# Layer 0 of a four-layer graph network on one core: in-degrees from packed adjacency tiles, and layer 3's weight products moved from the front into layer 0's steps

## The chip, the cores and the metric

The kernel runs on one core of one Trainium2 chip, in one launch. The metric is device time in microseconds, the median of several runs of the same kernel. A core has TensorE (PE; its weight loads are shown as PEld), VectorE (DVE), ScalarE (ACT), GpSimd (POOL) and SyncE (SP), which here issues most of the transfers. Each engine takes its instructions in the order in which they stand in its own queue, and waits on semaphores for the others.

## What is computed

The input is x, 2708 nodes by 512 features in f32, and a symmetric 0/1 adjacency matrix adj of 2708 by 2708 in int32, about 2.4% ones and a full diagonal. Four layers follow, each `x = x + layer(relu(layernorm(x)), adj)`. Cut to what matters:

```python
# layer 0
h = relu(layernorm(x));  a = adj.astype(f32)
out = (a.T @ h) @ W0
norm = clip(a.sum(axis=0), 1, None) ** -0.5        # in-degree of each node
x = x + relu(out * norm[:, None])
# layer 1: mean over the first 64 neighbours, two weight products, leaky relu
# layer 2: attention with 8 heads of 64
# layer 3
agg = mask @ h / max(deg, 1)
self_f, nb_f = h @ W_self + b_self, agg @ W_nb + b_nb
x = x + relu(concat(self_f, nb_f) @ W_comb + b_comb)
```

Layer 3 has no nonlinearity between its products, so W_self and W_nb can each be multiplied beforehand with their half of W_comb, and the biases b_self and b_nb too.

## The kernel before, in words

**Chunks and groups.** The 2708 nodes are NC = 22 chunks of 128 rows, the last of 20. The adjacency columns are cut into six groups of chunks, `sizes = [4, 4, 4, 4, 3, 3]`. A unit is a pair (g, m): the block of adjacency rows of chunk m and columns of group g, a tile `ai` of 128x512 (or 128x384) int32, 256 KB. There are 6 x 22 units in order.

**The steps of layer 0.** `staged` (L244) walks over the steps and runs a list of stages, each with a lag: at step s a stage with lag l works on unit s - l.

- lag 0, `load0` (L487): SP loads the adjacency block, into one of ten `ai` buffers.
- only in group 0, `dense` (L264): lag 0 loads the rows of x, lag 1 `norm` (L213: statistics and normalized `hn` on VectorE, the square root on ScalarE), lag 2 `relu_T` (L235: four transposes on TensorE, `hT` written out by ScalarE), lag 3 `product0` (L478): four f32 matmuls with W0, each of which leaves two records in the trace (tile `h_ps`, L186), and `halves` (L285), which splits the result into two parts, one by ScalarE, one by VectorE.
- lag 4, `count0` (L518): ScalarE turns `ai` into the f32 tile `ar` (L523); VectorE runs a scan along the rows (`cum`, L529), keeps the row's running degree (`deg`, L537), and for even m packs two blocks as low and high byte of an int16 tile `two` (L541), which has three buffers.
- lag 5, `sign0` (L553): ScalarE makes a sign count out of `cum` (L557).
- lag 7, `multiply0` (L567): GpSimd issues the store of `two` to the DRAM tile `packed` (L574). TensorE multiplies `ar` with the two halves of h into one PSUM accumulator `acc` for each chunk of the group (L403: 8 or 6 matmuls a unit).

`fenced` (L509) puts `count0` and `sign0` behind the last eviction of the group before, on the same engine. Apart from such edges and from data the build's scheduler decides the order of each queue.

**In-degrees.** For the column sums TensorE also multiplies a column of ones (`oneb`, 32 wide) with the upper 16-bit halves of every `ar` tile (L592), in batches of four tiles at m = 3, 7, 11, 15 and of six at m = 19. ScalarE copies the sums out (`by_col`, L601), and at m = 21 TensorE transposes them (L607), VectorE takes the maximum with 1 (L611), ScalarE the root (L618), VectorE the reciprocal `nrm` (L619). Then `acc` is evicted with that factor, alternately by ScalarE (L645) and VectorE (L640), and GpSimd adds it to x (L648) in all groups but the last.

**Layer 3's weights.** Ahead of all this stands a block of its own (L324 to L375): it loads W_self, W_comb and W_nb; TensorE transposes the two weights (`turn_weight`, L341) and multiplies them with W_comb (`fuse`, L347); VectorE copies the results out (L354); GpSimd stores each of the two as a whole to DRAM (L356). VectorE sums the biases times rows of W_comb into `part` (L367, L369), and TensorE adds over its partitions (L373). Then come the four loads of W0, and layer 0. Layer 3 reads the products much later (`load_l3_weights`).

PSUM has eight banks, shared by all these tiles (`ps`). At the change of group up to four old and four new accumulators exist. x tiles have five buffers.

## Time and profile before

| | before |
|---|---|
| median of 3 runs | 1802.83 us (1800.16 to 1804.46) |
| the profiled execution: time, span | 1800.19 us, 1798.3 us |
| TensorE busy | 1767.9 us, 98% |
| VectorE, ScalarE, GpSimd busy | 1309.7, 816.0, 248.7 us |
| mean granted TensorE clock | 0.995 |
| layer 0's first product; its last | starts at 39.04 us; ends at about 375.9 us |
| column sums (L592) | 484 matmuls from 77.9 to 372.0 us |
| products of layer 3's weights (L347) | 64 records from 7.4 to 36.2 us |

A line of the timeline is: start, duration, engine, source line, operation, written tile, read tiles, shape, number of instructions merged into it, and in brackets how long the engine had been idle and what ended it. A row of the windows is: the stretch, its length, the busy time of PE, PEld, DVE, ACT, POOL with the number of instructions, the granted clock of TensorE, the share of the DMA engines, GB/s. Durations of matmuls overlap in the pipeline, so their cost is read from start to start.

### The profile page before, as it was taken

The numbers are of one execution on the slowest core, as the hardware profiler recorded it, in microseconds if no ns is written. First come the engines' busy times: TensorE is split into PE (matmuls) and PEld (weight loads), VectorE is DVE, ScalarE is ACT, GpSimd is POOL, SyncE is SP. The second block draws the span as 40 slices with busy tenths as digits, with TensorE's granted clock in tenths as the row PEclk, the third lists the DMA queues.
The fourth block names the chain that finished last, engine by engine and source line by source line (L and its number), as shares of the span: only waits on it lengthen the run. The fifth ranks groups of instructions, "written<-read, shape, count | busy, mean of one in ns | idle before, by whom it ended". The sixth has DMA issues, their size and how long they took to land.

```text
span 1798.3 us, 30708 instructions
## 1 busy us (share of the span) xinstructions
PE 1767.9 (98%) x11880; PEld 1050.8 (58%) x11880; DVE 1309.7 (73%) x1842; ACT 816.0 (45%) x1554; POOL 248.7 (14%) x245
## 2 busy tenths in 40 slices
PE   9899999999999999999999999999999999999998
PEld 4456777654448888644454444444444455588786
DVE  4952998855446655888999999999999777633334
ACT  2643777732210000156887767767774566400000
POOL 0101332311111211266000000000001222100000
PEclk9999999999999999999999999999999999999999
DMA  7632666634451211243220121121022444313221
GB/s 251 199 106 71 210 204 192 205 80 119 122 142 50 69 55 47 86 147 123 74 62 25 45 63 44 27 63 50 19 68 60 141 134 133 107 43 99 71 71 40
DMA packets 166445, 176.06 MB, mean 98 GB/s; under 512 B 83454, under 2 KB 105918, under 8 KB 165394
## 3 DMA queue, kind: packets, MB, share of 16 engines
q1 hardware_dynamic: 143738, 130.61, 25.7%
q10 hardware_dynamic: 18808, 33.37, 4.9%
q0 software_dynamic: 3744, 10.03, 1.5%
q8 instruction: 95, 1.56, 0.4%
q14 instruction: 60, 0.49, 0.1%
HBM read 110.60 MB, written 55.36 MB: 92 GB/s over the span
## 4 chain that ended last, share of the span: by engine, by line
PE 86%; DVE 7%; issue 3%; DMA 3%; ACT 1%; POOL 1%; DVEq 0%; SPq 0%; ACTq 0%; POOLq 0%
PE acc L403 33%; PE av L1110 19%; PE nb_ps L186 8%; PE sums L1110 6%; PE wh_ps L186 4%; PE self_ps L186 4%; PE line_ps L186 4%; DVE t L923 3%; PE h_ps L186 3%; PE hT_ps L239 2%; PE fused_ps L347 2%; DVE cum L529 2%; DMA ai<-in_adj 1%; DMA degd<-deg 1%; PE av_ps L1063 1%
## 5 line engine op out<-in xcount | busy, mean ns | idle before, releaser
L923 DVE SCALAR_TENSOR_TENSOR t<-rb,ec,vT 128x2708 f32<-128x2708 f32 (+2 forms) x220 | 529.5, 2461 | 13.2 <-PE sums L1110 8.2
L1110 PE MATMUL av<-t,whs 128*32 128x451 f32 (+3 forms) x4576 | 436.7, 515 | 0.9 <-DVE ln_mv L218 0.9
L403 PE MATMUL acc<-halves,kt 128*128 128x512 f32 x1848 | 433.3, 394 | 2.4 <-DVE kt L777 2.1
L403 PEld LDWEIGHTS acc<-halves,kt 128*128 128x128 f32 x1848 | 345.8, 188 | 86.0 <-DVE kt L777 6.6
L1110 PEld LDWEIGHTS av<-t,whs 128*32 128x32 f32 (+1 forms) x4576 | 166.5, 110 | 198.3 <-issue 170.8
L403 PE MATMUL acc<-halves,ar 128*128 128x512 f32 x924 | 233.3, 405 | 3.3 <-ACT ar L523 2.4
L941 ACT ACTIVATE b<-t,eb 128x2708 bf16<-128x2708 f32 (+3 forms) x91 | 218.0, 2396 | 36.2 <-DVE t L923 34.6
L403 PEld LDWEIGHTS acc<-halves,ar 128*128 128x128 f32 x924 | 170.4, 188 | 52.5 <-issue 6.9
L777 DVE SCALAR_TENSOR_TENSOR kt<-lastr,index,vT 128x512 fp32r<-128x512 int16 (+3 forms) x154 | 111.4, 735 | 75.9 <-PE acc L403 75.5
L220 ACT ACTIVATE ln_rs<-ln_mv,eps 128x1 f32<-128x1 f32 x88 | 25.4, 292 | 295.0 <-DVE ln_mv L218 285.6
L1349 DVE CAST kt<-vT 128x512 fp32r<-128x512 uint8 (+3 forms) x154 | 56.4, 368 | 138.2 <-PE acc L403 138.2
L1077 POOL TENSOR_SCALAR z<-y 128x512 f32<-128x512 f32 x22 | 44.1, 2004 | 655.3 <-DVE y L1070 646.4
L1110 PE MATMUL sums<-t,whs 128*32 128x338 f32 (+4 forms) x1464 | 131.7, 449 | 0.8 <-ACT out L1151 0.8
L529 DVE TENSOR_TENSOR_SCAN cum<-ai,deg 128x512 int16<-128x512 int32 (+2 forms) x110 | 128.0, 1176 | 0.5 <-DMA ai<-in_adj 0.5
L911 ACT ACTIVATE whs<-wh,ef 128x64 f32<-128x64 f32 x220 | 76.5, 348 | 99.4 <-PE sums L1110 47.6
L557 ACT ACTIVATE cum<-cum,limit 128x512 int16<-128x512 int16 (+3 forms) x132 | 88.0, 667 | 55.8 <-DVE deg L537 54.9
L1110 PEld LDWEIGHTS sums<-t,whs 128*32 128x32 f32 (+1 forms) x1464 | 54.6, 109 | 62.2 <-issue 32.2
L216 DVE BATCH_NORM_STATS2 ln_st<-x 128x6 f32<-128x512 f32 x88 | 60.2, 684 | 35.6 <-DMA x<-x 22.5
L186 PE MATMUL h_ps<-w0s,hT 128*128 128x512 f32 x168 | 78.5, 611 | 2.3 <-DVE deg L537 1.4
L186 PE MATMUL nb_ps<-wfn,hT 128*128 128x512 f32 x168 | 78.5, 611 | 2.1 <-ACT hT L241 2.1
L241 ACT ACTIVATE hT<-hT_ps 128x512 f32<-128x512 f32 x88 | 51.8, 589 | 54.4 <-PE hT_ps L239 52.8
L523 ACT ACTIVATE ar<-ai 128x512 fp32r<-128x512 int32 (+2 forms) x132 | 74.9, 567 | 2.4 <-DMA ai<-in_adj 2.4
(202 smaller groups left out, 1911.9 us busy)
## 6 DMA issues: line engine op xcount, KB each, us to landing
x<-x SPq DMA_DIRECT2D x105, 256.0 KB
ai<-in_adj SPq DMA_DIRECT2D x84, 256.0 KB
x<-x ACTq DMA_DIRECT2D x84, 256.0 KB
x<-in_x SPq DMA_DIRECT2D x42, 256.0 KB
rb<-rT SPq DMA_DIRECT2D x7, 1354.0 KB
wh<-whd SPq DMA_DIRECT2D x70, 96.0 KB
packed<-two POOLq DMA_DIRECT2D x44, 128.0 KB, 3.7
whd<-wh SPq DMA_DIRECT2D x21, 256.0 KB
```

Of the source, the lines that this page charges most:

```text
L186: nc.tensor.matmul(po[:n], lhsT[:, f, :n], w[:, f, :], start=(f == 0), stop=(f == NF - 1))
L216: nc.vector.bn_stats(st[:n], xc[:n])
L403: nc.tensor.matmul(acc[:R], weight[:, k * R : (k + 1) * R], parts[:, i, :], start=(m == 0 and i == 0), stop=(m == NC - 1),)
L523: nc.scalar.activation(ar[:, :gw], ai[:, :gw], AF.Square, accum_out=squares[:R, m, g : g + 1])
L529: nc.vector.tensor_tensor_scan(cum[:n, :gw], ai[:n, :gw], ai[:n, :gw], 0.0 if g == 0 else deg[:n, m : m + 1], op0=ALU.add, op1=ALU.max,)
L557: nc.scalar.activation(cum[:n, :gw], cum[:n, :gw], AF.Sign, bias=limit[:n], scale=-1.0, accum_out=signs[:n, m, g : g + 1],)
L777: nc.vector.scalar_tensor_tensor(by_chunk(kt, cs), lastr[:, cs[0] * R : (cs[-1] + 1) * R].rearrange("p (c r) -> p c r", r=R), index[:R, m ...
L911: ins = nc.scalar.activation(t[:q, :O], wh.pop((u, m))[:q], AF.Copy, scale=by)
L923: ins = nc.vector.scalar_tensor_tensor(t[:q, : hi - lo], row[h][:q, lo:hi], ec[:q, m, h : h + 1], vT[g][:q, k, lo:hi], op0=ALU.max, op1=AL ...
L941: nc.scalar.activation(b[:q, : hi - lo], weight[s][:q, : hi - lo], AF.Sigmoid, bias=eb[:q, m, h : h + 1], scale=STEEP,)
L1110: nc.tensor.matmul(p[j * S : (j + 1) * S, : b - a], lhsT, rhs[:, part * size + a : part * size + b], start=(s % NC == 0), stop=(s % NC == ...
L1349: nc.vector.tensor_copy(by_chunk(kt, cs), pattern(m, cs))
```

## The change

Both parts lie in layer 0.

*In-degrees.* In `count0`, GpSimd adds up the packed tiles `two` of row chunks 0 to 18 of a group as 32-bit integers, one add for each even m from 2 on (tile `total`; no byte overflows with ten tiles of zeros and ones). At m = 20 VectorE adds the low and high bytes into a bf16 tile `by_row`. At m = 19 of the multiply stage TensorE multiplies, for each chunk of the group, three stationary tiles (`by_row` and the upper halves of the last two `ar` tiles) with one column of ones: 12 or 9 matmuls of one column a group, whose result stands with nodes on partitions, so that the copy and the transpose go. The maximum, root and reciprocal follow there and not at m = 21. `two` has four buffers.

*Layer 3's weights.* The block in front goes. SP issues x chunk 0, half of W_self, x chunk 1, the other half, and W0; TensorE transposes W_self there. W_comb's halves, W_nb and the biases are loaded in the steps, W_comb's first half and the biases from step 12 of group 0. The products go one matmul at a time into the steps of groups 1 and 2 (W_self), and the transposes and products of W_nb into those of groups 3 and 4. ScalarE, not VectorE, copies the products out, and each quarter is stored by itself. The bias row is summed by VectorE in the last steps ahead of groups 1 and 3 and closed in group 5. `count0` and `sign0` of the first 20 units also stand behind the normalized `hn` of the chunk two ahead (VectorE) and the `hT` of the chunk one ahead (ScalarE).

In the instruction queues as built, SP has the loads x0, ws, ws, x1, ws, ws, four w0s, then adjacency and x in turn, and W_comb's first half with the biases around x chunks 12 and 13. TensorE has 16 transposes of W_self, 8 of chunks 0 and 1, product 0, the transposes of chunk 2, product 1, and so on. VectorE has the first four bias operations behind the normalization of chunk 9 and in front of the halves of chunk 5.

```diff
@@ norm, relu_T
-        nc.vector.tensor_scalar(hn[:n], xc[:n], mv[:n, 0:1], rs[:n], ...)
+        normed.append(nc.vector.tensor_scalar(hn[:n], ...).ins)
...
+        evicted.append(nc.scalar.activation(hT[:, :, :n], pt[:, :, :n], AF.Relu).ins)
@@ front
-    with tc.tile_pool(name="pre", bufs=2) as pre:
-        ws = [load_weight(pre, w_self, "ws")]
-        wc = load_weight(pre, w_comb, "wc", k=2 * NF)
-        ws.append(load_weight(pre, w_nb3, "ws"))
...
-        turn_weight(0)
-        for f in range(NF):
-            if f == NF // 2:
-                turn_weight(1)
-            fuse(0, f)
-        for f in range(NF):
-            fuse(1, f)
...
+    class Fusion:
...
+        def turn(self, i, f):
+            if f == 0:
+                self.wsT[i] = self.pool.tile([P, NF, D], F32, name="wsT")
+            pt = ps.tile([P, NF, P], F32, name="wsT_ps", tag="ps")
+            for k in range(NF):
+                nc.tensor.transpose(pt[:, k, :], self.ws[i][:, f, k * P : (k + 1) * P], ident)
+            nc.scalar.copy(self.wsT[i][:, :, f * P : (f + 1) * P], pt)
+
+        def multiply(self, i, f, k):
+            if k == 0:
+                self.po[i, f] = ps.tile([P, D], F32, name="fused_ps", tag="ps")
+            po = self.po[i, f]
+            nc.tensor.matmul(
+                po,
+                self.wsT[i][:, k, f * P : (f + 1) * P],
+                self.wc[i][:, k, :],
+                start=(k == 0),
+                stop=(k == NF - 1),
+            )
+            if k == NF - 1:
+                wf = self.pool.tile([P, D], F32, name="wf", bufs=1)
+                nc.scalar.copy(wf, self.po.pop((i, f)))
+                nc.gpsimd.dma_start(fused[i][f * P : (f + 1) * P, :], wf)
@@ fenced
-                        for ins in fences.values():
+                        early = ()
+                        if i < NC - 2:
+                            early = normed[i + 2], evicted[i + 1]
+                        for ins in (*fences.values(), *early):
@@ count0
-                    two = wk.tile([R, WG + P - R], I16, name="two", bufs=3)
+                    two = wk.tile([R, WG + P - R], I16, name="two", bufs=4)
...
+                    if m == 0:
+                        pairs[g] = two
+                    elif m < NC - 2:
+                        total = pairs[g]
+                        if m == 2:
+                            total = wk.tile([R, WG], I16, name="total", bufs=1)
+                        nc.gpsimd.tensor_tensor(
+                            total[:, :KR].bitcast(I32),
+                            pairs[g][:, :KR].bitcast(I32),
+                            two[:, :KR].bitcast(I32),
+                            ALU.add,
+                        )
+                        pairs[g] = total
+                    else:
+                        both = pairs.pop(g)[:, :KR].bitcast(mybir.dt.uint8)
+                        both = both.rearrange("p (w e) -> p e w", e=2)
+                        by_row = by_rows[g] = wk.tile([R, WG], BF16, name="by_row", bufs=1)
+                        nc.vector.tensor_tensor(by_row[:, :KR], both[:, 0], both[:, 1], ALU.add)
@@ multiply0
-                for j in batch:
-                    q = rows(j)
-                    for k in range(K):
-                        nc.tensor.matmul(
-                            sums[g][k * 32 : (k + 1) * 32, :R],
-                            oneb[:q],
-                            uppers[j][:q, 2 * k * R + 1 : 2 * (k + 1) * R : 2],
...
+                if m == NC - 3:
+                    by_row = by_rows.pop(g)
+                    uppers = [(by_row, 1, R)]
+                    uppers += [(tiles[i + j][0].bitcast(BF16), 2, rows(m + j)) for j in (1, 2)]
+                    pt = ps.tile([P, KMAX], F32, name="sums_ps", tag="ps")
+                    for k in range(K):
+                        for j, (upper, e, q) in enumerate(uppers):
+                            nc.tensor.matmul(
+                                pt[:R, k : k + 1],
+                                upper[:q, e * k * R + e - 1 : e * (k + 1) * R : e],
+                                oneb[:q, :1],
+                                start=(j == 0),
+                                stop=(j == len(uppers) - 1),
+                            )
@@ the steps
+            def load_first(i):
...
+                load(0)
+                fusion.load_ws(0, half=0)
+                load(1)
+                fusion.load_ws(0, half=1)
+                w0_of.append(load_weight(weights, w0, "w0s", tag="w"))
+                for f in range(NF):
+                    fusion.turn(0, f)
...
+            for i in range(2):
+                first_unit = (1 + 2 * i) * NC
+                at(first_unit - 10, fusion.load, i)
+                steps = [(fusion.turn, i, f) for f in range(NF) if i]
+                steps += [(fusion.multiply, i, f, k) for f in range(NF) for k in range(NF)]
+                for g, own in enumerate((steps[: len(steps) // 2], steps[len(steps) // 2 :])):
+                    for n, step in enumerate(own):
+                        at(first_unit + g * NC + 2 + n * (NC - 5) // len(own), *step)
+                for k in range(NF):
+                    at(first_unit - 4 + k, fusion.add, i, k)
+            at(5 * NC + 2, fusion.close)
...
             staged(
                 len(units),
+                (0, load_first),
                 (0, load0),
-                *[first_dense(lag, fn) for lag, fn in dense(x_in, product0, rows_of=paired)],
+                *first[1:],
                 (4, fenced(count0)),
                 (5, fenced(sign0)),
                 (7, save0),
                 (7, multiply0),
+                (7, fuse0),
             )
```

## The prediction

> **What bounds the kernel now.** I read the page's busy line first, then the stretches of layer 0 (windows), then TensorE's timeline at the two places where it idles, then the rows of the pieces that the change touches.
>
> ```profile
> PE 1767.9 (98%) x11880; PEld 1050.8 (58%) x11880; DVE 1309.7 (73%) x1842; ACT 816.0 (45%) x1554; POOL 248.7 (14%) x245
> ...
> 39.00:164.00 125.00, 120.38 (x462) 67.83 (x464) 72.39 (x146) 57.09 (x147) 9.46 (x18) 0.97 0.41 133
> ...
> 173.70:216.90 43.20, 43.20 (x263) 33.36 (x262) 39.52 (x59) 32.16 (x92) 13.37 (x16) 1.00 0.66 205
> ...
> 303.20:340.80 37.60, 34.26 (x199) 25.12 (x197) 31.65 (x64) 26.84 (x92) 13.32 (x19) 1.00 0.55 172
> 340.80:375.90 35.10, 34.02 (x203) 25.69 (x202) 26.10 (x82) 22.12 (x87) 11.66 (x22) 1.00 0.40 115
> ```
>
> TensorE is busy 1767.9 of 1798.3 us, so moving work that it must still do gains only what it now idles or runs slowly; only removing work gains more. In layer 0 (rows: length, then PE, PEld, DVE, ACT, POOL busy, clock, DMA) it idles 4.6 us in group 0 with its dense steps (125.0 - 120.38), nothing in groups 1 to 3 (43.2 us each, VectorE at 39.5), 3.3 in group 4 and 1.1 in group 5. The front:
>
> ```profile
> 3.64 3.88 PE L341 MATMUL wsT_ps<-ident,ws 128*128 128x128 f32 x16 [3.64 <-DMA ws<-in_L_gnn_W_self]
> ...
> 14.30 1.91 PE L341 MATMUL wsT_ps<-ident,ws 128*128 128x128 f32 x16
> ...
> 16.05 20.77 PE L347 MATMUL fused_ps<-wc,wsT 128*128 128x512 f32 x48
> ...
> 39.04 3.70 PE L186 MATMUL h_ps<-w0s,hT 128*128 128x512 f32 x8 [0.25 <-ACT hT L241]
> ```
>
> The first product of layer 0 starts at 39.04. A matmul of these weights has two records: 20.77/24 = 0.865 us each, 32 of them 27.7 us. Later in group 0 TensorE waits for a normalized chunk that stands behind scans on VectorE:
>
> ```profile
> 82.84 1.11 PE L239 MATMUL hT_ps<-ident,hn 128*128 128x128 f32 x4 [2.50 <-DVE deg L537]
> 84.29 6.14 PE L186 MATMUL h_ps<-w0s,hT 128*128 128x512 f32 x8 [0.34 <-ACT hT L241]
> ...
> 86.00:88.00 2.00, 2.00 (x4) 0.80 (x3) 2.00 (x5) 0.41 (x1) 0.00 (x0) 0.50 0.35 135
> ```
>
> VectorE is busy all of that row, and the clock granted after the 2.5 us wait is 0.50: the eight records take 6.14 instead of 3.6 us, the transposes 1.11 instead of 0.60, so 3.0 us more are lost.
>
> **The part taken away: column sums on TensorE.** One batch of four tiles costs the gap between two products:
>
> ```profile
> 222.67 0.42 PE L592 MATMUL sums_ps<-ar,oneb 128*32 128x128 bf16 x16
> 223.02 1.20 PE L403 MATMUL acc<-halves,ar 128*128 128x512 f32 x4
> ...
> 211.55 0.64 PE L592 MATMUL sums_ps<-ar,oneb 128*32 128x128 bf16 x24
> 212.12 3.99 PE L403 MATMUL acc<-halves,ar 128*128 128x512 f32 x16
> ```
>
> Start to start: 0.35 us for 16, 0.57 for the last 24. A group has four of the first and one of the second, and one transpose of 0.11: 2.08 us, in the three-chunk groups (0.34 for 12) 2.04. Six groups: 12.4 us.
>
> In their place stand 66 pairs of a 128-column weight load and a one-column matmul (12 in a four-chunk group, 9 in the others). No row of before has that pair. Below: 0.35/16 = 0.022 us a pair, as the 32-column loads show (1.5 us in all). Above: 0.11, the pace of the L239 transposes (four in 0.44 us), which load 128 columns too (7.3 us); if each waited out its own load and its result, as rows of small matmuls with 0.19 + 0.18 us durations have it, 24 us. I take 0.08, near the transposes because the load has their width but half their bytes: 5.3 us. Net -7.1 us.
>
> GpSimd gets nine adds a group (54) of 128x256, or 128x192, int32. The nearest row is its own add of 128x512 f32:
>
> ```profile
> L648 POOL TENSOR_TENSOR x<-x,y x19: 1283/1702/2210, 175.5 to 345.9; 128x512 f32<-128x512 f32 x19
> ...
> 307.06 3.27 DVE L529 TENSOR_TENSOR_SCAN cum<-ai,deg 128x384 int16<-128x384 int32 x2
> ...
> 310.30 1.53 DVE L541 SCALAR_TENSOR_TENSOR two<-ai 128x384 int16<-128x384 int32 x1
> ```
>
> Half of 1702 ns is 0.85 us, 7.7 a group; below 0.6, above 1.7 if the integer form costs double. With the page's 13.4 us a group and the packed stores in the same queue GpSimd stays under half busy, and nothing that it feeds is due before the by_row add of row chunk 20, two chunks after the last sum: free on GpSimd. But these adds slow VectorE. While four adds ran from 305.07 to 311.41, two scans took 3.27 instead of 1.91 us and a pack 1.53 instead of 0.54: 2.4 us lost in 6.3, a share of 0.38, or 2.9 us a group. The Trainium skill (SBUF — State Buffer, section on the two separate sides) makes it harsher: the pair that VectorE and GpSimd share is an exclusive lock for a whole instruction, against a VectorE op with two SBUF inputs too, so all 7.7 us would be lost. The trace shows longer scans, not full exclusion. By the trace VectorE needs 39.5 + 2.9 + 0.6 (by_row, at a pack's price) = 43.0 us in groups 1 to 3, by the rule 47.8. TensorE there will need 43.2 - 2.1 + 1.0 + 6.9 (eight products) = 49.0 (group 3: six products and 1.9 us of transposes, 49.2). So both cost nothing behind the moved products; without that cover (42.1 us) the rule would cost 5.7 us a group, the trace 0.9. Group 4: VectorE 31.65 + 0.5 + 2.2 to 5.8, under TensorE's 34.3 + 8.7 - 1.3. Group 5 has no products: 26.1 + 0.5 + 2.2 to 5.8 = 28.8 to 32.4 against 34.
>
> The divisor is now made at row chunk 19, so the 0.9 us chain transpose, max, root, reciprocal before the evictions goes. TensorE did not wait for it: zero.
>
> **The part moved: layer 3's weights.** In front stay 16 transposes of W_self (1.9 us), done while layer 0's weights come in. Into groups 1 to 4 go the 32 products (27.7), 16 transposes (1.9) and into group 5 the bias product (0.9): 30.5 us of TensorE, none hidden, since groups 1 to 3 have no gap. VectorE loses eight evictions of 0.68 us to ScalarE (0.58 each; it has 11 us a group free). The partial bias (four ops of 0.7) stands on VectorE inside the dense steps and waits for the combining weights and bcol, which SP issues right behind x chunk 13. In before bcol landed some 4 us after its issue; VectorE's 9 us of work since the release of chunk 13 cover that. Behind it queue the halves of chunk 5, which TensorE wants two steps later: zero, at most 2 us if the cover fails. SP's 22 issues (8 ws, 8 wc, biases) go in among x and adjacency loads at 0.5 us each, with steps of 6 us: zero. GpSimd's eight stores, 0.54 to 0.99 us, stand before packed stores; nothing waits. An accumulator bank for a product is wanted at row chunk 2, some 4 us after the group's start, by when the old four are evicted (last at 220.04 for a group that ended at 216.9): 0 to 1 us a group, in the allowance below.
>
> **The new front.** SP issues x0, half of ws, x1, half of ws, four w0s. Before, loads 5 to 8 (wc) were taken up at 7.33, 7.98, 8.73 and 9.59; w0s is now loads 7 to 10, so the first product starts at about 8.7 instead of 39.04. In the order of the built kernel the transposes of chunk 2 stand before product 1; x2 is load 12, lands near 11.5 to 12, and its chain (statistics 0.69, 0.17, root 0.29, 0.15, normalize 0.54, hand-overs) ends near 14.2, while product 0 ends near 12.2: a wait of 2.0. After that the new fences put a scan behind the normalize of the chunk two ahead, and VectorE's step of 3.9 us (2.2 dense, 1.7 count) fits into TensorE's 6: the 4.6 us of waits and 3.0 of slow clock go.
>
> Here a rule speaks against the change. At its start the trace shows a clock of 1.00 from the first transpose on after 3.6 us without work. The Trainium skill (TensorE: Matmul & The Clock Gate, Part 1) has half rate as the default and after an idle window of about 3.4 us, and a warm-up of about 3.4 us. The old front warmed up on work that had to wait for nothing; the new one has sparse transposes and a 2 us wait at 12. By the trace's start it costs 0; by the rule, and by 82.8 to 89.3, up to 3.0. I take 1.5.
>
> **The sum,** on the profiled execution (span 1798.3, time 1800.19). From the first product (39.04) to layer 0's last (375.94): 336.9 us. Less idle 4.6 + 3.3 + 1.1, clock 3.0, sums 12.4: 312.5. Plus pairs 5.3, moved work 30.5: 348.3. Plus new losses: wait at chunk 2 2.0, clock 1.5, groups 1 to 5 together 1.5: 353.3. From 8.7 on, layer 0 ends at 362.0 instead of 375.9: 13.9 us less. Nothing behind it changes. On the profiled run 1786.3, on the median 1802.83, which is 2.6 higher, 1788.9. The profiled one is at the fast end of 1800.16 to 1804.46, so I say 1788.
>
> **The rivals.** (A) As above, 62%: 1782 to 1794 from the pair at 0.022 to 0.11 and losses of 2 to 10 us. (B) The front starves, 16%: x and adjacency share SP, VectorE hits the partial bias too early, a wait of 3 us or more brings the half clock several times; two such spells at 2.5 + 3.0 (as at 82) take 5 to 11 us back: 1794 to 1801. For it: one such wait now costs that; against it: the new fences. (C) Slower, 5%: the integer adds on GpSimd shut VectorE out. Its slack after by_row is 8.8 us in each of groups 1 to 3, 9.4 in group 4, 7.0 in group 5; at a blocked time b per wide add (three quarters of it per narrow one) the excess is 27b - 26.4 + 13.5b - 16.4, the whole gain of 13.9 from b = 1.40 us. At 1.7 (full-size row, wholly exclusive) it takes 26 us: 1814. Against it: 0.85 from the row and the 0.38 share. (D) More, 14%: pairs at 0.03, no slow clock, no wait at chunk 2: 1776 to 1782. (E) The change moves nothing in time, 3%: pairs pay the whole of 12.4 us and the front's start is lost to loads: 1800 to 1805.
>
> About 0.2% (3.6 us) is what a measurement of this kernel can tell from no change. Faster: A, D and 14 of B's 16: 0.90; same: 2 of B and E: 0.05; slower: C: 0.05. Range 1779 to 1797: A, 8 of D's 14 and 10 of B's 16, so 8 in 10.
>
> **What would show it.** The first h_ps record near 9 us; a gap of about 2 us before chunk 2's transposes; no wait on L561 in group 0, clock 1.00 past 15 us. L630: start to start 1.0 us for 12 pairs. Groups 1 to 3 at 49 us with PE full and VectorE at 43 to 48; group 4 about 42, group 5 about 34. GpSimd's L581 near 0.85 us. Layer 0's last product near 362. Wrong if L581 takes over 1.4 us with scans stretched alike, if the L630 pairs take over 0.2 us, or if the first dense steps show clock 0.50 for over 5 us.

## The result, and the profile after

| | before | after |
|---|---|---|
| median (range), same chip | 1803.12 us (1800.16 to 1804.46) | 1793.95 us (1792.77 to 1796.16) |
| ratio, 95% interval | | 0.9953 [0.994, 0.9966] |
| the profiled execution: time, span | 1800.19, 1798.3 us | 1793.95, 1792.2 us |
| layer 0's first product starts | 39.04 us | 11.15 us |
| layer 1's first product (`nb_ps`) starts | 376.32 us | 363.06 us |
| layer 1's aggregation (`acc<-halves,kt`) starts | 536.84 us | 531.04 us |

The change saves about 9 us, where 14.8 were forecast (1788; range 1779 to 1797). In the two profiles, layer 0 ends 13.3 us earlier, close to the forecast 13.9. Then 7.5 us are given back between layer 1's first product and its aggregation (160.52 us before, 167.98 after), and what follows takes the same time (1261.5 and 1261.2 us).

The busy line of after's page, and its windows by group (rows: stretch, length, busy time of PE, PEld, DVE, ACT, POOL with instructions, clock, DMA share, GB/s):

```profile
PE 1755.0 (98%) x11456; PEld 1044.4 (58%) x11456; DVE 1323.0 (74%) x1840; ACT 815.7 (46%) x1555; POOL 301.0 (17%) x305
```

```profile
11.15:135.70 124.55, 124.43 (x448) 73.56 (x449) 80.71 (x170) 60.82 (x162) 14.46 (x23) 1.00 0.50 163
135.70:183.90 48.20, 48.20 (x201) 35.99 (x200) 43.03 (x61) 32.75 (x93) 23.86 (x27) 1.00 0.64 201
183.90:232.10 48.20, 48.20 (x201) 36.02 (x201) 40.57 (x57) 30.50 (x86) 23.84 (x27) 1.00 0.68 211
232.10:288.70 56.60, 50.61 (x213) 37.83 (x212) 47.95 (x70) 36.15 (x104) 23.48 (x26) 0.97 0.52 164
288.70:329.60 40.90, 39.90 (x160) 28.66 (x159) 34.17 (x67) 28.42 (x98) 22.05 (x31) 1.00 0.59 185
329.60:362.60 33.00, 32.58 (x144) 24.78 (x144) 29.71 (x81) 21.39 (x83) 20.68 (x34) 1.00 0.48 140
362.60:392.00 29.40, 23.92 (x61) 11.02 (x60) 12.03 (x30) 5.30 (x12) 1.87 (x3) 0.88 0.35 80
```

Groups 0, 1 and 2 have TensorE full at clock 1.00. Two rows stand out: group 3 (232.10 to 288.70), where TensorE idles 6.0 us, and the first 29 us of layer 1, where it idles 5.5 us at a clock of 0.88. These are the two places to explain.

**Group 3.** TensorE's timeline, and VectorE's at the same place:

```profile
235.58 0.73 PE L423 MATMUL acc<-halves,ar 128*128 128x512 f32 x2 [1.89 <-DVE nrm L638]
...
249.27 3.63 PE L423 MATMUL acc<-halves,ar 128*128 128x512 f32 x8 [3.76 <-ACT ar L547]
```

```profile
232.31 3.15 DVE L387 SCALAR_TENSOR_TENSOR part<-wc,bcol,part 128x512 f32<-128x512 f32 x4 [4.94 <-DMA wc<-in_L_gnn_W_comb]
235.37 0.15 DVE L638 TENSOR_SCALAR nrm<-sums_ps 128x4 f32<-128x4 f32 x1
...
242.36 5.29 DVE L553 TENSOR_TENSOR_SCAN cum<-ai,deg 128x512 int16<-128x512 int32 x2
```

The second half of the partial bias (W_nb's four operations, L387) waits 4.94 us for W_comb's second half, which SP issues only at 227.66 us, behind eleven adjacency loads. The divisor (L638) is queued behind it. It reads `sums_ps` and so frees that bank of PSUM. TensorE has by then issued six products, two for each of three new accumulators, while group 2's four are not yet evicted: the fourth new one waits 1.89 us for the divisor. The evictions queue behind it too, and VectorE is then late: two scans next to GpSimd's four additions to x take 5.29 us (two such scans without neighbours: 2.43 us, at 235.89), ScalarE's sign counts wait for them with `ar` behind, and TensorE waits 3.76 us more, after which eight products take 3.63 us at half clock instead of 2.13. At the start of group 1 the same scans take 5.29 us too (at 139.95) and TensorE waits for nothing; there VectorE was not late.

**Layer 1's start.** VectorE, then ScalarE, then TensorE, in after:

```profile
372.61 0.18 DVE L758 TENSOR_SCALAR rcnt<-rdeg 128x22 f32<-128x22 f32 x1 [12.76 <-DMA rdeg<-degd]
...
373.38 0.45 DVE L233 TENSOR_SCALAR hn<-x,ln_mv,ln_rs 128x512 f32<-128x512 f32 x1
```

```profile
373.94 0.20 ACT L641 ACTIVATE nrm<-nrm 128x3 f32<-128x3 f32 x1 [13.96 <-DVE nrm L638]
```

```profile
373.89 0.66 PE L244 MATMUL hT_ps<-ident,hn 128*128 128x128 f32 x4 [3.80 <-DVE hn L233]
376.22 6.70 PE L186 MATMUL nb_ps<-wn,hT 128*128 128x512 f32 x8 [1.68 <-ACT hT L246]
```

and VectorE and TensorE at the same place before:

```profile
381.22 0.18 DVE L695 TENSOR_SCALAR rcnt<-rdeg 128x22 f32<-128x22 f32 x1 [12.40 <-DMA rdeg<-degd]
```

```profile
383.63 3.60 PE L186 MATMUL nb_ps<-wn,hT 128*128 128x512 f32 x8
...
392.38 0.66 PE L239 MATMUL hT_ps<-ident,hn 128*128 128x128 f32 x4 [1.28 <-DVE hn L230]
```

The node degrees go to DRAM and come back in another layout (`degd`, `rdeg`), for the divisors of layers 1 and 3 (`rcnt`, four small operations). VectorE meets them right after layer 0's last scans and waits 12.4 us before, 12.8 after. The third `hn` of layer 1 (chunk 2) is queued behind, and TensorE's first wait (3.80 us) is for it. Layer 0's last divisor is queued there too: ScalarE waits 13.96 us for it, with the `hT` of layer 1's chunk 1 behind, and that is TensorE's second wait (1.68 us). Before, VectorE started its last scan at 366.6 us and TensorE still had 9.3 us of layer 0 to do (to 375.9). After, it starts that scan at 357.65 with TensorE at 5.0 us from the end (362.6). The wait is as long; its cover has shrunk. Idle 3.80 + 1.68 and, at half clock, 6.70 instead of 3.60 us: 8.6 us, against 1.28 before; the difference, 7.3, is the 7.5 given back.

### The profile page after: what moved, and what is told of

It reads as the page before. It is cut to its first block, busy times and chain, and to the rows that moved or that the text cites. A ratio compares the mean times of both kernels' runs of the same rounds, so it can differ in the third digit from the quotient of the medians.

```text
span 1792.2 us, 29931 instructions
## 1 busy us (share of the span) xinstructions
PE 1755.0 (98%) x11456; PEld 1044.4 (58%) x11456; DVE 1323.0 (74%) x1840; ACT 815.7 (46%) x1555; POOL 301.0 (17%) x305
## 4 chain that ended last, share of the span: by engine, by line
PE 82%; DVE 9%; DMA 3%; issue 3%; ACT 1%; POOL 1%; SPq 0%; DVEq 0%; POOLq 0%; ACTq 0%
PE acc L423 31%; PE av L1173 19%; PE nb_ps L186 8%; PE sums L1173 6%; PE self_ps L186 4%; PE line_ps L186 4%; PE wh_ps L186 3%; DVE t L986 3%; PE h_ps L186 3%; DVE cum L553 2%; PE hT_ps L244 2%; PE fused_ps L369 1%; DMA x<-in_x 1%; DMA degd<-deg 1%; DMA ai<-in_adj 1%
## 5 line engine op out<-in xcount | busy, mean ns | idle before, releaser
L423 PE MATMUL acc<-halves,ar 128*128 128x512 f32 x924 | 249.3, 420 | 7.4 <-ACT ar L547 5.0
L553 DVE TENSOR_TENSOR_SCAN cum<-ai,deg 128x512 int16<-128x512 int32 (+2 forms) x110 | 143.2, 1318 | 0.0
L186 PE MATMUL nb_ps<-wn,hT 128*128 128x512 f32 x168 | 78.7, 612 | 1.7 <-ACT hT L246 1.7
L186 PE MATMUL wh_ps<-w2s,hT 128*128 128x512 f32 x168 | 75.8, 593 | 0.0
```

The source lines that it names most:

```text
L186: nc.tensor.matmul(po[:n], lhsT[:, f, :n], w[:, f, :], start=(f == 0), stop=(f == NF - 1))
L423: nc.tensor.matmul(acc[:R], weight[:, k * R : (k + 1) * R], parts[:, i, :], start=(m == 0 and i == 0), stop=(m == NC - 1),)
L553: nc.vector.tensor_tensor_scan(cum[:n, :gw], ai[:n, :gw], ai[:n, :gw], 0.0 if g == 0 else deg[:n, m : m + 1], op0=ALU.add, op1=ALU.max,)
```

## The experiments

Each ratio is against the kernel before on the same chip, with its 95% interval. The first four runs, the next four and the last three each shared a chip.

| kernel | median us | ratio to before |
|---|---|---|
| W_nb's bias operations later | 1788.26 | 0.9934 [0.992, 0.9949] |
| divisors `rcnt` later | 1789.55 | 0.994 [0.9925, 0.9955] |
| both moves | 1781.19 | 0.9898 [0.9883, 0.9912] |
| before, with `rcnt` later | 1799.33 | 0.9995 [0.9986, 1.0003] |
| the change again | 1795.0 | 0.9966 [0.9955, 0.9977] |
| in-degree part alone | 1815.33 | 1.0084 [1.007, 1.0099] |
| front part alone | 1788.03 | 0.9932 [0.9918, 0.9945] |
| the change without the early fences | 1805.84 | 1.0028 [1.0018, 1.0039] |
| both moves, again | 1778.91 | 0.9879 [0.9864, 0.9894] |
| front part alone, both moves | 1786.8 | 0.9924 [0.991, 0.9937] |
| the change, GpSimd's adds left out | 1783.11 | 0.9893 [0.9878, 0.9909] |

### The two waits of VectorE, each moved

**W_nb's bias operations later** (12 units later, and behind group 2's evictions on VectorE):

```diff
+            def add_behind(i, k):
+                with tc.issue_after(fences["dve"]):
+                    fusion.add(i, k)
...
-                    at(first_unit - 4 + k, fusion.add, i, k)
+                    at(first_unit - 4 + k + 12 * i, add_behind if i else fusion.add, i, k)
```

> The changed kernel with one edit: the four bias operations of W_nb's half are traced twelve units later and stand on VectorE behind the evictions at the start of group 3. Theory W (VectorE waits 4.94 us for the second half of W_comb, and the divisor and evictions of group 2 queue behind it): group 3 falls from 56.6 to 48 to 49 us, no half clock there, and the time falls by 6 to 9 us against the changed kernel's 1794, to about 1786. Rival G (the integer adds on GpSimd shut VectorE out in group 3): group 3 stays over 54 us and the time within 2 us of 1794. Rival L (the gain is given back at the start of layer 1, where TensorE waits for the row degrees anyway): group 3 is short, but the time falls by under 3 us.

Measured: layer 1's first product starts at 355.77 instead of 363.06 us. The stall in group 3 is gone (0.81 us of waiting is left); the waits at layer 1's start are there as in the change (3.76 and 1.67 us, then eight products in 6.43).

**The divisors `rcnt` later** (their four operations stand behind the normalization of layer 1's chunk 8):

```diff
-        nc.vector.tensor_scalar(rcnt, rdeg, float(NEIGHBORS), 1.0, op0=ALU.min, op1=ALU.max)
-        nc.vector.reciprocal(rcnt, rcnt)
-        nc.vector.tensor_scalar(rdeg, rdeg, 1.0, None, op0=ALU.max)
-        nc.vector.reciprocal(rdeg, rdeg)
...
         staged(NC, *stages1, done=len(AHEAD))
+        with tc.issue_after(normed[NC + 8]):
+            nc.vector.tensor_scalar(rcnt, rdeg, float(NEIGHBORS), 1.0, op0=ALU.min, op1=ALU.max)
+            nc.vector.reciprocal(rcnt, rcnt)
+            nc.vector.tensor_scalar(rdeg, rdeg, 1.0, None, op0=ALU.max)
+            nc.vector.reciprocal(rdeg, rdeg)
```

> The changed kernel with one edit: the four VectorE operations that turn the row degrees into rcnt and rdeg stand behind the normalization of layer 1's chunk 8. Theory D (VectorE waits 12.8 us for the round trip of the degrees through DRAM, and the normalization of layer 1's chunk 2 queues behind it, after which TensorE runs at half clock): the waits of 3.80 and 1.68 us and the slow products (6.70 instead of 3.60) at 374 to 383 us go, and the time falls by 6 to 8 us, to 1786 to 1788. Rival X (the x1 rows of layer 1 are late anyway): TensorE waits elsewhere between 370 and 400 us and the time falls by under 3 us.

Measured: layer 0 ends as in after (layer 1's first product at 362.70), the wait is gone, and layer 1's aggregation starts at 522.42 instead of 531.04 us.

**Both moves:**

> Both edits together: bias operations of W_nb behind the evictions of group 2, and rcnt and rdeg behind layer 1's chunk 8. If W and D are separate waits, the gains add: 13 to 16 us below the changed kernel, 1778 to 1781. If one gives the other back, it is within 3 us of the better of the two single edits.

**Before, with the divisors later:**

> The kernel before with the edit on rcnt and rdeg alone. Theory D says that the same 12.4 us wait on VectorE costs almost nothing there, because TensorE still has 7 to 9 us of layer 0 left when it begins: only the 1.28 us idle before chunk 3's transposes can go, so 1801.5 to 1803.5, no change. If instead it gains over 4 us, the wait was costly before as well, and the changed kernel did not uncover it.

Measured up to the start of layer 1's aggregation, the moves save 7.6 us (523.44), 8.6 us (522.42) and together 15.5 us (515.51): they add, so these are two separate losses. The divisors' move leaves the kernel before unchanged (0.9995), although the wait that it removes is just as long there: before, it was covered. So the loss in layer 1 is due to the cover that the change took away, not to the wait as such. The whole times say it less cleanly. Against the change's ratios of 0.9953 and 0.9966 (the change did not run on this chip), W_nb's move gains 3 to 6 us where 6 to 9 were expected, the divisors' 2 to 5 where 6 to 8 were, and both 10 to 12 where 13 to 16 were.

The profiled executions show where a part of the gain goes. From the aggregation's start to the end those of the two single moves need some 1266.5 us, those of after, of before and of both moves 1261 to 1263. Of the 5 us to after, 3.5 lie in layer 2's attention (from its first product to layer 3's first: 555.9 and 555.8 us, against 552.4). It is the clock. TensorE has the same waits there, one of 2.49 us and later two of 0.94 and 1.83, but more half clock follows them in the single moves. Around the first the clock is 0.83 in after (986 to 996 us) and 0.66 in W_nb's move (979 to 989); around the other two, after and then W_nb's move:

```profile
1380.00:1389.02 9.02, 6.25 (x83) 2.92 (x75) 7.81 (x17) 5.79 (x10) 2.42 (x2) 1.00 0.23 69
1374.50:1385.45 10.95, 8.19 (x82) 3.38 (x74) 9.70 (x19) 5.91 (x10) 4.36 (x3) 0.81 0.29 83
```

The remaining 1.7 us are a product of layer 3 that takes 5.40 instead of 3.70 us after a wait (one as slow, 5.25 us, stands in both moves). Two executions of one and the same kernel differ in this way too (after, in its second run, shows a clock of 1.00 at the first of these waits), so this is no loss that the moves are shown to cause.

The windows of both moves (second run; group 3, layer 1's start):

```profile
232.10:281.20 49.10, 48.30 (x214) 36.84 (x213) 45.20 (x69) 34.15 (x97) 24.12 (x26) 1.00 0.58 186
355.20:385.00 29.80, 29.71 (x84) 13.78 (x82) 14.79 (x31) 5.96 (x13) 3.11 (x3) 1.00 0.50 108
```

Group 3 takes 49.10 us, as the prediction had it, and layer 1 starts with TensorE full.

### One part alone, and the fences

**The change again:**

> The changed kernel without any edit, on the chip on which the parts are timed, as their common reference. From its ratio of 0.9953 it stands 8.4 us below the kernel before, with group 3 at 56 to 57 us and the wait at layer 1's chunk 2 again.

Measured: 6.1 us below before, not 8.4; the two intervals overlap. The waits are much the same (1.84, 0.22 and 3.75 us in group 3, 3.92 and 1.22 at layer 1's start).

**The in-degree part alone** (the kernel before, with the GpSimd adds, `by_row` and the one-column products; the weights stay in front, no early fences):

```diff
-                    two = wk.tile([R, WG + P - R], I16, name="two", bufs=3)
+                    two = wk.tile([R, WG + P - R], I16, name="two", bufs=4)
...
+                        nc.gpsimd.tensor_tensor(
+                            total[:, :KR].bitcast(I32),
+                            pairs[g][:, :KR].bitcast(I32),
+                            two[:, :KR].bitcast(I32),
+                            ALU.add,
+                        )
...
-                for j in batch:
...
+                if m == NC - 3:
+                    by_row = by_rows.pop(g)
```

> The kernel before with the in-degree part alone (adds on GpSimd, one-column matmuls, four buffers of two). There the moved products no longer cover VectorE. Theory S (a share of about 0.38 of GpSimd's add time is lost on VectorE): VectorE needs some 43 us in groups 1 to 3, TensorE only 41.4, so these groups stay at 42.5 to 43.5 us, and the time falls by 2 to 6 us from group 0, 4 and 5. Rival R (the shared pair is locked for whole instructions): groups 1 to 3 take 47 us or more and the time rises by 5 us or more. Rival F (adds cost VectorE nothing): groups at 41.4 us and the time falls by 9 to 11 us.

Its windows (group 0 with the dense steps, then groups 1 to 3, which lasted 43.2 us each before):

```profile
39.00:174.00 135.00, 128.58 (x449) 75.05 (x450) 74.38 (x150) 59.88 (x157) 20.78 (x26) 0.97 0.41 130
174.00:218.20 44.20, 42.07 (x186) 32.84 (x185) 41.00 (x60) 30.45 (x86) 22.82 (x25) 1.00 0.63 201
218.20:265.00 46.80, 42.99 (x185) 34.15 (x185) 43.60 (x61) 32.34 (x94) 22.81 (x25) 0.96 0.63 197
265.00:312.60 47.60, 44.25 (x185) 35.06 (x185) 44.38 (x66) 32.98 (x96) 22.81 (x25) 0.93 0.60 183
```

TensorE has less to do and the groups get longer: it now waits for ScalarE's `ar` (12.2 us in all of layer 0, the longest 3.8), which comes behind VectorE's scans, and runs part of the time at a lower clock. VectorE's queue shows the bound. These are all its longer waits in one round from an eviction to the same eviction of the next group:

```profile
223.75 0.75 DVE L641 TENSOR_SCALAR y<-acc,nrm 128x512 f32<-128x512 f32 x1 [2.03 <-POOL x L649]
252.32 0.69 DVE L569 TENSOR_TENSOR by_row<-total 128x512 bf16<-128x512 uint8 x1 [0.56 <-POOL total L558]
264.16 0.18 DVE L620 RECIPROCAL nrm<-nrm 128x4 f32<-128x4 f32 x1 [0.27 <-ACT nrm L618]
270.09 0.75 DVE L641 TENSOR_SCALAR y<-acc,nrm 128x512 f32<-128x512 f32 x1 [2.03 <-POOL x L649]
```

A round takes 46.3 us (the one before it, from 177.40, too): 43.1 of work and 3.2 of waiting, nearly all of it for GpSimd and none for TensorE. So groups and time come out near what rival R said (47 us or more, the time up), but not by R's 7.7 us of lost VectorE time a group. With the wait at layer 1's start grown too (165.6 us to the aggregation instead of 160.5), the part by itself makes the kernel 14 us slower.

**The front part alone** (the change with before's column sums: no GpSimd adds, `two` with three buffers):

```diff
-                        nc.gpsimd.tensor_tensor(
-                            total[:, :KR].bitcast(I32),
...
-                if m == NC - 3:
-                    by_row = by_rows.pop(g)
...
+                for j in batch:
+                    q = rows(j)
+                    for k in range(K):
+                        nc.tensor.matmul(
+                            sums[g][k * 32 : (k + 1) * 32, :R],
+                            oneb[:q],
```

> The changed kernel with the column sums of before (484 matmuls on TensorE, divisor at row chunk 21, two with three buffers), so the moved weight products and the new front alone. The front still gains some 8 us (first product at 11 instead of 39 us, 30.5 us of products later, the waits and the half clock of group 0 gone), the stall of group 3 remains at 6 to 9 us, TensorE has some 11 us more to do, and is later at layer 1, so that the wait for the row degrees shrinks to under 3 us. Together 0 to 4 us below the kernel before. If the sums part was the whole gain, it is slower than before by 2 us or more.

```profile
137.20:187.30 50.10, 50.10 (x280) 36.43 (x279) 39.15 (x59) 33.22 (x94) 14.44 (x18) 1.00 0.61 194
187.30:237.20 49.90, 49.90 (x279) 36.28 (x278) 42.26 (x63) 33.21 (x94) 14.43 (x18) 1.00 0.68 216
```

The expectation (0 to 4 us below before) failed: it is 13 us below. Its wide groups take 50.0 us, 1.8 more than the change's, all on TensorE. Yet it beats the whole change by 7 us (1788.03 and 1795.0 on one chip), because group 3 has no stall (50.0 us as well) although VectorE waits 3.6 us for W_comb there too, and layer 1's start costs 161.1 us instead of 168. Without the adds VectorE is far enough ahead to afford both waits.

**The change without the early fences:**

```diff
-                        if i < NC - 2:
-                            early = normed[i + 2], evicted[i + 1]
```

> The changed kernel without the two new fences (a scan may stand ahead of the normalization two chunks on). If these fences removed the waits of group 0 (1.4, 2.5 us and 3.0 us of half clock in before), waits for normalized chunks come back in the first 120 us and the time rises by 3 to 8 us against the changed kernel. If the order of the loads alone did it (x and adjacency in turn, so that scans are not ready in a bunch), group 0 still takes 124 to 126 us and the time is within 1.5 us of the changed kernel.

The expected waits came back, and cost more than the 3 to 8 us expected. The first product starts at 13.55 us, and the window of group 0 has 5 us without work:

```profile
13.55:147.10 133.55, 128.31 (x449) 75.05 (x450) 80.55 (x168) 61.15 (x160) 19.19 (x23) 0.97 0.45 144
```

Group 0 takes 133.55 us instead of 124.55. The two fences are worth 11 us, more than the whole change brings: without them it would be slower than before (1.0028).

### The square, and the adds by themselves

**Both moves again, and the front part alone with both moves:**

> The whole change with both moves (W_nb's four bias operations later, the divisors rcnt/rdeg of layers 1 and 3 later). Theory: the two waits of VectorE are what the change lost; without them the time is about 1781, 12 to 14 us below the change, and layer 1's aggregation starts near 515.5. Rival (the gain of the two moves is chance of one chip): 1787 to 1790.

> The front part alone (column sums on TensorE as in before) with the same two moves. This completes a square of four: in-degree part yes or no, moves yes or no. Theory: without GpSimd's adds VectorE has a lead of its own and the moves are worth little, about 1.5 us, to some 1786.5; the in-degree part, worth minus 7 without the moves, is then worth plus 5 to 9 us with them (1.8 us of TensorE a wide group). Rival (the in-degree part costs more than it brings in any case): 1776 to 1780, below the whole change with the moves.

| ratio to before | without the moves | with both moves |
|---|---|---|
| front part | 0.9932 | 0.9924 |
| front and in-degree part | 0.9966 | 0.9879 |

The moves are worth 1 us where there are no adds (the intervals overlap), and 10 to 16 us where there are (0.9953 and 0.9966 to 0.9898 and 0.9879). The in-degree part costs 7 us without the moves and brings 8 us with them (1786.8 to 1778.91). The version with both parts and both moves is the fastest of all that ran: 1778.91 us.

**The change without GpSimd's adds** (`by_row` from the last packed tile alone):

```diff
                     elif m < NC - 2:
-                        total = pairs[g]
-                        if m == 2:
-                            total = wk.tile([R, WG], I16, name="total", bufs=1)
-                        nc.gpsimd.tensor_tensor(
-                            total[:, :KR].bitcast(I32),
-                            pairs[g][:, :KR].bitcast(I32),
-                            two[:, :KR].bitcast(I32),
-                            ALU.add,
-                        )
-                        pairs[g] = total
+                        pairs[g] = two
```

> The whole change, with GpSimd's nine adds a group left out: by_row is made from the last packed tile alone, so the in-degrees lack rows 0 to 2303; all the rest is as in the change. Theory (the adds stretch VectorE's scans and so use up its lead): scans of 128x512 go back from 1.52 to about 1.34 us, the wait for W_comb's second half ahead of group 3 stays at 3 to 5 us but costs TensorE 0 to 3 us instead of 8.7, the wait of layer 1's start is covered as in before; 1783 to 1788. Rival 1 (the two waits are there whatever the adds do): 1792 to 1796. Rival 2 (GpSimd shuts VectorE out for whole adds, 7.7 us a group): VectorE's busy time in groups 1 and 2 falls from 43 to about 35 us rather than to 40.

The scans from 130 to 360 us by shape (count, then busy time and mean ns of one), before, after, and with the adds left out:

```profile
L529 DVE TENSOR_TENSOR_SCAN cum<-ai,deg 128x512 int16<-128x512 int32 x60 | 79.3, 1337 | 0.0
```

```profile
L553 DVE TENSOR_TENSOR_SCAN cum<-ai,deg 128x512 int16<-128x512 int32 x62 | 93.1, 1520 | 0.0
```

```profile
L553 DVE TENSOR_TENSOR_SCAN cum<-ai,deg 128x512 int16<-128x512 int32 x62 | 81.4, 1332 | 0.0
```

1520 ns with the adds, 1337 and 1332 without: the adds stretch a wide scan by 0.18 us in the mean, 4.0 us a group of 22. Its windows of groups 1 to 3:

```profile
135.60:183.60 48.00, 48.00 (x201) 36.11 (x201) 39.43 (x62) 32.97 (x93) 14.47 (x18) 1.00 0.64 202
183.60:231.60 48.00, 48.00 (x201) 36.09 (x200) 40.13 (x62) 31.38 (x89) 14.45 (x18) 1.00 0.71 223
231.60:281.20 49.60, 48.47 (x213) 36.70 (x213) 41.24 (x66) 35.42 (x103) 13.91 (x17) 1.00 0.57 176
```

VectorE still waits for W_comb (5.6 us in all), but group 3 loses 1.1 us of TensorE instead of 6.0. VectorE's load in group 1 falls from 43.0 to 39.4 us, not to 35: rival 2 took 0.85 us for each add, which is twice what an add costs VectorE (the part on the prediction shows it). Layer 1's start is only partly cured (1.03 and 1.68 us of waits, the clock stays full), which the expectation had not allowed for. In groups 1 and 2, behind the moved products, the adds cost TensorE 0.2 us each. Of their price of 12 us in the whole change (1795.0 and 1783.11, with before at 1801.1 and 1801.2) most is paid at the two waits: 7.0 us in group 3, 4.2 at layer 1's start.

How long after layer 1's first product `rcnt` runs orders these kernels:

| kernel | layer 1's first product to `rcnt` | to its aggregation |
|---|---|---|
| before | 4.9 us | 160.5 us |
| front part alone | 5.2 us | 161.1 us |
| the change, adds left out | 6.8 us | 163.8 us |
| the change | 9.5 us | 168.0 us |

The front part, with the sums still on TensorE, keeps before's lead of VectorE. Taking the sums off TensorE costs 1.6 us of it (6.8 against 5.2), the adds 2.7 more.

## Why the prediction was right, and where it was not

The time lies in the range and the forecast direction is right; the size is 6 us short. By its own steps:

- **First product at 8.7 us: it started at 11.15.** The step counted when W0 would land, not what stands in TensorE's queue ahead of product 0: the sixteen transposes of W_self and eight of chunks 0 and 1. The former waited for the loads of W_self, and they ran at half speed:

```profile
4.26 1.08 PE L362 MATMUL wsT_ps<-ident,ws 128*128 128x128 f32 x4 [4.26 <-DMA ws<-in_L_gnn_W_self]
6.27 1.12 PE L362 MATMUL wsT_ps<-ident,ws 128*128 128x128 f32 x4 [0.93 <-DMA ws<-in_L_gnn_W_self]
7.73 1.97 PE L362 MATMUL wsT_ps<-ident,ws 128*128 128x128 f32 x8 [0.34 <-DMA ws<-in_L_gnn_W_self]
9.49 1.41 PE L244 MATMUL hT_ps<-ident,hn 128*128 128x128 f32 x8
11.15 3.70 PE L186 MATMUL h_ps<-w0s,hT 128*128 128x512 f32 x8 [0.25 <-ACT hT L246]
```

  Four transposes take 1.08 and 1.12 us here and 0.60 later (at 18.69); the eight at 7.73 take 1.76 us from start to start, half of W_self's sixteen at 14.30 in before 0.87. With the eight of the chunks (1.41 us, at full speed 1.09 in before) some 1.2 of the 2.4 us of delay are clock (an estimate from these rows).
- **A wait of 2.0 us at chunk 2 and 1.5 us of slow clock.** The wait did not come: product 0 started later, and chunk 2 was ready (its transposes start at 14.76 without a wait). The slow clock came, ahead of product 0 and not after it, and 1.5 us was a fair size for it. The prediction had read "a clock of 1.00 from the first transpose on" off the windows. Its own lines speak against that: the first sixteen transposes of W_self take 3.88 us, the second sixteen 1.91. The column says 1.00 because the trace holds no record of the clock before 7.32 us (10.24 in after), where the pace doubles. So the rule that the prediction quotes against the change holds at the start. In other executions of the new front full speed came later still: product 0 took 4.23 us in the change again and 4.73 in the first run of both moves, instead of 3.70.
- **Group 0** ends 124.6 us after the first product, where the steps give 129.5 (134.7 before, less 4.6, 3.0 and 2.08, plus 0.96, 2.0 and 1.5). The fences, which the prediction costed at 7.6 us of removed waits, are worth 11.
- **Column sums: the pairs are right, what they replace was under-sized.** Twelve pairs take 132.82 - 131.86 = 0.96 us, 0.08 each:

```profile
131.86 0.18 PE L630 MATMUL sums_ps<-oneb,by_row 128*128 128x1 bf16 x1
131.90 0.27 PE L630 MATMUL sums_ps<-oneb,ar 128*128 128x1 bf16 x2
...
132.82 1.43 PE L423 MATMUL acc<-halves,ar 128*128 128x512 f32 x5
```

  The wide groups with before's sums take 50.0 us and with the pairs 48.2, so the sums cost 1.8 + 0.96 = 2.8 us, not the 2.08 read from start to start. That gap in the timeline did not hold all of their price.
- **Moved products, 30.5 us, none hidden: right.** Eight products make a wide group 50.0 - 43.2 = 6.8 us longer (6.9 in the sum).
- **VectorE's loss to the adds: exclusion, but of short adds.** The scans lose 4.0 us a group, between the 2.9 of the trace's share and the 7.7 of the rule. The prediction says that "the trace shows longer scans, not full exclusion", and that does not hold for single records. A scan, an add, the next scan (group 1 of after):

```profile
145.87 1.27 DVE L553 TENSOR_TENSOR_SCAN cum<-ai,deg 128x512 int16<-128x512 int32 x1
146.03 1.64 POOL L581 TENSOR_TENSOR total<-total,two 128x256 int32<-128x256 int32 x1 [3.05 <-DVE deg L561]
147.06 1.70 DVE L553 TENSOR_TENSOR_SCAN cum<-ai,deg 128x512 int16<-128x512 int32 x1
```

  The first scan is not stretched. The add, issued during it, ends 0.53 us after it (0.73 us alone), and the next scan ends 1.09 us after the add. They go one after the other, as the exclusive lock of the Trainium skill has it (SBUF — State Buffer, section on the two separate sides), and an add costs VectorE 1.70 - 1.27 = 0.43 us; at that price nine cost 3.9 (an estimate). What was wrong is the 0.85 us for an add: it is half of a median of 1702 ns that itself holds such waits; the f32 adds that wait for nothing take 1283. So rival C had the right kind of wait and three times its size: 0.43 us lost per add, with the bound at 1.40. VectorE's busy time in groups 1 and 2, 43.03 and 40.57 us, is at or below the forecast 43.0.
- **"Without that cover the rule would cost 5.7 us a group, the trace 0.9": the in-degree part alone lost 2.1, 4.7 and 5.5 us** over TensorE's 42.1. This step failed, and it is the one to learn from: it compared busy times. VectorE was busy for 43.1 us a round and yet its round took 46.3, since it also waits, above all for GpSimd (2.03 us for the buffer of `y`, 0.56 for `total`). The mean excess of the three groups, 4.1 us, is 46.3 less 42.1.
- **The partial bias, "zero, at most 2 us": 7.5 us.** The step looked at the first half, ahead of chunk 5's halves, and there it held. It left out the second half of the same code ahead of group 3, where the divisor and the evictions stand behind it. Group 3 took 56.6 us instead of 49.2; with the move 49.1. The wait alone does not do it: without the adds it is there and costs about 1 us. An estimate says why: with the adds VectorE needs its round of 46.3 us and 3.0 more for these four operations, as much as TensorE's 49.1, so it cannot catch up in group 3.
- **Group 4 at about 42, group 5 about 34: 40.7 and 33.2.**
- **Layer 0's end, 362.0 against 362.8 us measured, is right by errors that cancel.** Group 0 came out 5 us better, groups 1, 2, 4 and 5 some 3 better, and the 1.5 allowed for groups 1 to 5 was not needed; the first product was 2.4 later and group 3 cost 7.4 more.
- **"Nothing behind it changes" failed, and makes up the missing gain.** Shortening layer 0 on TensorE by more than on VectorE shrinks VectorE's lead at its end, from 9.3 to 5.0 us, and that lead covered the 12.4 us wait for `rdeg`. Before's trace showed the wait on VectorE, and 1.28 us of idle TensorE behind it. Both moves together restore what the prediction had promised and more: 1778.91 to 1781.19 us.

## What to carry to other kernels

Follow every wait of a second engine that the bounding engine does not feel, and write down how long its cover lasts: a change that shortens the bounding engine's stage, or loads the second engine, uses up that lead and uncovers the wait further on, even in another stage. When two parts are changed together, run the square of both: here one part alone slowed the kernel by 0.8%, cost 7 us on top of the other, and gained 8 us once two waits in front of it had been moved. Where operations come in two halves at two places, cost each place with what is queued behind it. Compare the rounds of two engines and not their busy times: an engine's waits for a third one belong to its round. And before calling it sharing that two engines slow each other, look at single records: a mean, or a pair merged into one line, hides who waits for whom.

## What the runs showed of the hardware

- A scan of VectorE and an add of GpSimd (all their inputs in SBUF) run one after the other when they meet. In before, with f32 adds of 128x512, each ends 1.08 or 1.09 us after the one above it:

```profile
177.50 1.63 DVE L529 TENSOR_TENSOR_SCAN cum<-ai,deg 128x512 int16<-128x512 int32 x1
178.01 2.21 POOL L648 TENSOR_TENSOR x<-x,y 128x512 f32<-128x512 f32 x1
179.06 2.24 DVE L529 TENSOR_TENSOR_SCAN cum<-ai,deg 128x512 int16<-128x512 int32 x1
180.18 2.21 POOL L648 TENSOR_TENSOR x<-x,y 128x512 f32<-128x512 f32 x1
```

- Which of them gets in first is not fixed. In after the scan issued at 242.36 was held up by two adds in a row, until the last one's end at 245.38, and took 4.12 us; the pair lost 2.86 us. VectorE's evictions out of PSUM took 0.75 us next to such adds (before, 306.40) and without them (304.18).
- A GpSimd int32 add of 128x256 takes 0.73 us where no scan runs (239.11) and 1.64 where it is issued during one.
- TensorE starts at half speed: sixteen transposes take 3.88 us at the start of before and 1.91 later. Full speed came at 7.32 us there, 3.7 us after the first transpose, and at 10.24 in after, 6.0 us after it, where the transposes came with gaps.
- Later, half clock came after single waits of 2.50 us (before, at 82.84) and 3.76 us (after, at 249.27). The length of a wait does not decide it alone: without the early fences products of the same form after nearly the same wait ran at full and at half clock,

```profile
56.73 3.67 PE L186 MATMUL h_ps<-w0s,hT 128*128 128x512 f32 x8 [2.63 <-DVE deg L559]
65.32 5.37 PE L186 MATMUL h_ps<-w0s,hT 128*128 128x512 f32 x8 [2.61 <-DVE deg L559]
```

  and of two waits with four transposes between, 3.80 and 1.68 us were followed by half clock (6.70 us), 1.03 and 1.68 by full (3.70 us).
